# A convolution stage whose opening is reordered: reciprocals from a small column, extra TensorE work, and the first sequence run through by itself

## The chip, the cores and the metric

The kernel runs on one core of a Trainium2 chip. The metric is device time in microseconds (us); ten runs of the kernel before gave a median of 1289.62 us, the lowest 1288.46, the highest 1291.89. Five engines work side by side, each through its own list of instructions in order: TensorE (PE in the profile; its weight loads are PEld), VectorE (DVE), ScalarE (ACT), GpSimd (POOL) and SyncE (SP, which here only issues DMA transfers). An engine waits on semaphores that other engines and the DMA queues raise.

## The reference

Four stages run one after the other over an array x of 8 sequences by 512 tokens by 128 features: an attention-like dynamic convolution, an FFN with weights and inputs rounded to a 4-bit format, a test-time-training attention, and a mixture of experts. Each stage adds its result to x. The change lies in the first stage only:

```python
x = layernorm(x)                                     # per token, eps 1e-5
avg = cumsum(x, axis=1) / arange(1, l + 1)           # running mean over tokens
ci  = avg in 16 heads of 8 features                  # (b*H, l, 8)
dyn, gate = split(ci @ W_pe + b_pe)                  # 31 + 31 numbers per head and token
w = softmax(stt_energy + sigmoid(gate) * dyn)        # over 31 taps, each head and token
out[t] = sum_k w[t, k] * ci[t - 30 + k]              # causal, 31 taps
v = out @ W_fc.T + x
x_in + layernorm(v, eps 1e-6) * gamma + beta
```

## The kernel before

`sequence_conv` is the first stage. It treats the eight sequences (b = 0 to 7) one after the other, each as four tiles of 128 tokens; features or (head, tap) pairs lie on the partitions, the 512 tokens along the free axis. 31 taps are held as four groups g = 0 to 3 of eight.

The steps for one sequence, with the helper that issues them and its line in the kernel before:

- `norm0` (statistics at L255 and L257, root, offset at L270) and `scaled` (L274): the layer norm. Sequences 0 and 1 take their root with ACT's Sqrt (L268), the others with a chain of 14 small DVE operations (`rsqrt`, L85 to L93).
- `means` (L285, copy at L288): running mean. Four matmuls multiply the normed tokens by `tri`, a 512 by 512 triangle that holds 1/(t+1). Two DMA steps on SP's queue (`far` L291, `base` L294) then lay the mean out again, shifted by taps.
- `gates` (matmul eg at L300, Tanh L309, Copy L310) and `taps` (matmul ev at L300): the sigmoid of the gate and the dynamic part, two groups at a time, `half_` being 0 or 1.
- `energy` (L325 writes en, L329 and L331 keep the running maximum `top`), `turn_top`, `greatest` (L341, L343), `turn_greatest`, `less` (L351): energies, their maximum over taps, and its subtraction. `weigh` (L362, L364): exponentials.
- `part_sums`, `sums`, `invert` (L384): the softmax's denominator.
- `shared` (L402, POOL) and `product` (L411, DVE): weights times shifted means, six of eight features on DVE and two on POOL. `add_up` (cv): PE sums over taps into one PSUM bank.
- `scale_down`, `project`, `norm1`, `finish`: projection, second norm (a Newton chain on POOL for all but the last sequence), gamma, addition to x. `add_beta` (L460): x plus beta on POOL, any time after `scaled`.

A loop over b holds the steady work. Iteration b multiplies sequence b, and between its products works ahead on b+1 and b+2 and finishes b-1 and b-2. A prologue ahead of the loop fills this pipeline: it takes sequence 0 to its exponentials, sequence 1 to its first two energies and all its gates, and sequence 2 to its mean, and has all norms done.

The order on the engines is mostly written out by hand: the helpers `vec`, `ten`, `act` and `gp` each chain an instruction behind the one issued before through the same helper, so the program's text fixes the order of what passes through them. Instructions that don't pass through a helper are placed by the framework. Before, `add_beta` on POOL is of that kind.

Setting up, POOL makes `inv` (token numbers, L174), which DVE turns into reciprocals (L175, 128x512), the head mask (L180, L183), `by_k` (L230, biases in another order, from two small DMAs into `rows`), `tri` (four selects, L190), `wbig` (a memset, L210, and eight products, L214), and `half` (L236). ACT's queue issues the small input DMAs, and from `by_k` the DMA of `bias` (L232); SP's queue loads x in eight pieces.

PSUM pools: `ps_e` has two banks for eg and ev; `ps_m` one for means, turns and sums; `ps_c` one for cv; `ps_p` one for the projection; `ps_w` three for the exponentials of groups 0 to 2.

Of the kernel before, what the change touches and what calls it, by code (L numbers as in the profile page):

```python
# [7 lines left out]
F32 = mybir.dt.float32  # L8
# [132 lines left out]
def sequence_conv(cx):  # L141
# [17 lines left out]
    PITCH = PAD + L + 2  # L159
    with ExitStack() as st:  # L160
# [11 lines left out]

        inv = wp.tile([P, L], F32, tag="inv", name="inv")
        nc.gpsimd.iota(inv, [[1, L]], base=1, channel_multiplier=0, allow_small_or_imprecise_dtypes=True)  # L174
        vec(nc.vector.reciprocal(inv, inv))  # L175
# [11 lines left out]

        tri = wp.tile([P, G, L], F32, tag="tri", name="tri")
        for j in range(G):
            gp(nc.gpsimd.affine_select(  # L190
                out=tri[:, j, :], in_=inv, pattern=[[1, L]], compare_op=ALU.is_ge, fill=0.0,
                base=-P * j, channel_multiplier=-1,
            ))
# [15 lines left out]
        wbig = wp.tile([P, 2, NGR, H, KK], F32, tag="wbig", name="wbig")  # L209
        nc.gpsimd.memset(wbig, 0.0)  # L210
        for s in (1, 0):
            for g in range(NGR):
                n = min(KK, KC - KK * g)
                gp(nc.gpsimd.tensor_tensor(  # L214
                    wbig[:, s, g, :, :n],
                    wrep[:, s * KC + KK * g : s * KC + KK * g + n].unsqueeze(1).to_broadcast([P, H, n]),
                    mask_h.unsqueeze(2).to_broadcast([P, H, n]),
                    ALU.mult,
                ))
# [6 lines left out]
        with nc.allow_non_contiguous_dma(reason="small biases, once"):  # L226
# [3 lines left out]
        nc.gpsimd.tensor_copy(by_k.rearrange("h k s g -> h s g k"), rows.rearrange("h s (g k) -> h s g k", k=KK))  # L230
        bias = wp.tile([P, 3, NGR], F32, tag="bias", name="bias")
        nc.scalar.dma_start(  # L232
            out=bias.rearrange("p s g -> p (s g)"), in_=by_k.rearrange("h k s g -> h (k s g)")
        )
        half = wp.tile([P, NGR], F32, tag="half", name="half")
        gp(nc.gpsimd.tensor_scalar(half, bias[:, 1, :], 0.5, None, ALU.mult))  # L236
        wfc = wp.tile([P, D], F32, tag="wfc", name="wfc")
        nc.scalar.dma_start(out=wfc, in_=ins["L0_attn_W_fc"])
        wfc_p = wp.tile([P, NJ, ND, H], F32, tag="wfc_p", name="wfc_p")
        nc.gpsimd.tensor_copy(  # L240
            wfc_p.rearrange("p j i h -> p h i j"), wfc.rearrange("p (h i j) -> p h i j", h=H, i=ND)
        )
        wfc_t = wp.tile([P, D], F32, tag="wfc_t", name="wfc_t")
        gamma = cx.bcast(wp, "L0_attn_gamma", D)
        beta = cx.bcast(wp, "L0_attn_beta", D)

# [12 lines left out]
        def norm0(lo, hi):  # L259

            at = slice(lo * G, hi * G)
            for b in range(lo, hi):
                stats(grp(cx.x, b), mv0[:, b * G : (b + 1) * G, :])
            rs = rs0[:, at]
            if lo:
                rsqrt(nc, wp, mv0[:, at, 1], 1e-5, rs, (hi - lo) * G, vec)
            else:
                act(nc.scalar.activation(rs, mv0[:, at, 1], AF.Sqrt, bias=cx.eps[1e-5]))  # L268
                vec(nc.vector.reciprocal(rs, rs))
            vec(nc.vector.scalar_tensor_tensor(off0[:, at], mv0[:, at, 0], -1.0, rs, ALU.mult, ALU.mult))  # L270
# [7 lines left out]
        def means(b):  # L278

            avg = p2.tile([P, PITCH], F32, tag="avg", name="avg", bufs=3)  # L280
            nc.gpsimd.memset(avg[:, :PAD], 0.0)
            nc.gpsimd.memset(avg[:, PAD + L :], 0.0)
            av = ps_m.tile([P, L], F32, tag="m", name="av")
            for j in range(G):
                ten(nc.tensor.matmul(  # L285
                    av[:, j * P :], xn[:, b * G + j, :], tri[:, j, j * P :], start=(j == 0), stop=(j == G - 1)
                ))
            act(nc.scalar.copy(avg[:, PAD : PAD + L], av))  # L288
            base = p2.tile([P, DH, LB], F32, tag="base", name="base")
            far = dram.tile([P, PITCH], F32, tag="far", name="far")  # L290
            nc.sync.dma_start(out=far, in_=avg)  # L291
            for d in range(DH):
                src = bass.AP(far.tensor, far.offset + d * PITCH, [[DH * PITCH, H], [1, KK], [1, LB]])
                last = nc.sync.dma_start(out=base[:, d, :], in_=src)  # L294
            return dict(b=b, avg=avg, base=base, spread=last)

        def spread(s, i, g, name):
            e = ps_e.tile([P, L], F32, tag="e", name=name)
            now = s["avg"][:, PAD : PAD + L]
            ten(nc.tensor.matmul(e, wbig[:, i, g].rearrange("p a b -> p (a b)"), now, start=True, stop=True))  # L300
            return e

        def gates(s, half_):

            s["sg"] = {}
            for g in (2 * half_, 2 * half_ + 1):
                e = spread(s, 1, g, "eg")
                s["sg"][g] = sg = p2.tile([P, L], F32, tag="sg", name="sg", bufs=4)
                act(nc.scalar.activation(sg, e, AF.Tanh, bias=half[:, g : g + 1], scale=0.5))  # L309
                act(nc.scalar.activation(sg, sg, AF.Copy, bias=0.5, scale=0.5))  # L310

        def taps(s, half_):

            s["ev"] = {g: spread(s, 0, g, "ev") for g in (2 * half_, 2 * half_ + 1)}

        def values(s, half_):
            gates(s, half_)
            taps(s, half_)
# [139 lines left out]
        def add_beta(b):  # L458
            x = grp(cx.x, b)
            nc.gpsimd.tensor_tensor(x, x, beta.unsqueeze(1).to_broadcast([P, G, D]), ALU.add)  # L460


        norm0(0, 2)
        scaled(0)
        warm = wp.tile([P, 1], F32, tag="warm", name="warm")
        act(nc.scalar.activation(warm, cx.eps[1e-5], AF.Tanh))
        seq = {0: means(0)}
        gates(seq[0], 0)
        scaled(1)
        taps(seq[0], 0)  # L470
        norm0(2, 5)
        for g in (0, 1):
            energy(seq[0], g)
        values(seq[0], 1)
# [3 lines left out]
        seq[1] = means(1)  # L478
        for g in (2, 3):
            energy(seq[0], g)  # L480
        turn_top(seq[0])
        values(seq[1], 0)
        greatest(seq[0])
        turn_greatest(seq[0])
        scaled(2)
        norm0(5, B)
        for g in (0, 1):
            energy(seq[1], g)
        less(seq[0])
        gates(seq[1], 1)  # L490
        weigh(seq[0], 0, 1)
        seq[2] = means(2)
        taps(seq[1], 1)
        weigh(seq[0], 1, NGR)
        scaled(3)
        for b in range(B):
# [10 lines left out]
            add_up(cur, 0)  # L507
            if nxt:
                for g in (2, 3):
                    energy(nxt, g)  # L510
# [15 lines left out]
            if old:  # L526
                norm1(old, nc.gpsimd)
            if b + 4 < B:
                scaled(b + 4)
            product(cur, 2)  # L530
            add_up(cur, 2)
# [963 lines left out]
```

## Time and profile before

| what | value |
| --- | --- |
| median of ten runs | 1289.62 us |
| the profiled execution, its own time | 1292.55 us |
| its span in the profile | 1290.8 us |
| mean granted TensorE clock | 0.953 of full |
| first product on DVE (L411), sequence 0 | 45.23 us |
| first product of sequences 1, 2, 3, 4, 5 | 71.08, 97.83, 124.17, 150.51, 175.85 us |
| last product of sequence 7 begins | 239.80 us |
| busy over the whole span: PE, DVE, ACT, POOL | 85%, 59%, 38%, 57% |

A line of the timeline shows start, duration, engine, source line, operation, what it writes and reads, and how many alike were merged; a bracket at its end tells how long the engine was idle before and what ended that. A line of the windows shows, for a stretch of time, each engine's busy time with instruction counts, then the granted TensorE clock, the DMA share and GB/s. The convolution takes about the first 256 us of the span.

### The profile page before, as it was taken

The page shows a single profiled execution, that of the slowest core. Times are in us where ns is not written, and L with a number is a line of the kernel's source. Part 1 is how long each engine was busy: PE and PEld are TensorE (multiplying, and loading weights), DVE is VectorE, ACT ScalarE, POOL GpSimd, SP SyncE. Part 2 cuts the span into 40 slices and gives each one's busy share as a digit, 9 for nine tenths or more (in the row PEclk, how much of TensorE's full clock was granted, in tenths as well). Part 3 has the DMA queues.
Part 4 walks back from the last instruction along what each step waited for, and adds up shares of the span by engine and source line. Part 5 has one row for each costly group of instructions (what it writes and reads, how often), then busy time and mean ns, then how long its engine had stood idle before and what let it go on. Part 6 is the DMA issues. An engine that isn't in the chain of part 4 may idle for free.

```text
span 1290.8 us, 15323 instructions
## 1 busy us (share of the span) xinstructions
PE 1094.4 (85%) x5211; PEld 648.6 (50%) x5211; DVE 755.2 (59%) x1742; ACT 493.9 (38%) x1005; POOL 741.7 (57%) x724
## 2 busy tenths in 40 slices
PE   5899997546876699999998999999999991999990
PEld 2333442224655345555556455555576661676770
DVE  6899999687985544444445444444456873222234
ACT  4656555155556522222234223222343330333330
POOL 4347756635554688888840888888401665354542
PEclk9899999868999999999999999999999995899995
DMA  5223426660000000000000000000000112112137
GB/s 158 77 78 107 123 79 198 225 204 1 1 1 1 0 1 1 1 1 1 1 1 1 1 0 1 0 1 1 1 1 7 44 43 65 45 55 65 50 107 206
DMA packets 61615, 63.07 MB, mean 49 GB/s; under 512 B 6768, under 2 KB 44479, under 8 KB 61537
## 3 DMA queue, kind: packets, MB, share of 16 engines
q1 hardware_dynamic: 54016, 52.37, 13.8%
q0 software_dynamic: 4608, 8.43, 2.1%
q10 hardware_dynamic: 2912, 1.29, 0.5%
q8 instruction: 41, 0.67, 0.2%
q14 instruction: 38, 0.30, 0.1%
HBM read 37.90 MB, written 25.04 MB: 49 GB/s over the span
## 4 chain that ended last, share of the span: by engine, by line
PE 49%; DVE 13%; issue 5%; ACT 5%; POOL 5%; DMA 2%; SPq 0%; POOLq 0%; DVEq 0%; ACTq 0%
PE ph L1135 5%; PE sum L1110 4%; PE pp L1125 4%; PE sum L1109 4%; PE sum L1111 4%; PE pa L1087 4%; PE po L1420 4%; PE pb L1089 4%; PE ph L1411 4%; PE pt L1118 2%; PE gu L692 2%; POOL res L1435 1%; POOL v L619 1%; DVE ht L915 1%; PE a L975 1%
## 5 line engine op out<-in xcount | busy, mean ns | idle before, releaser
L1100 POOL TENSOR_TENSOR ds<-sw,s 128x512 f32<-128x512 f32 x64 | 81.5, 1274 | 87.1 <-DVE sw L1095 87.1
L1435 POOL DMA_INDIRECT res<-ye,xe x70 | 68.1, 973 | 88.6 <-DVE ye L1433 34.6
L1102 POOL TENSOR_TENSOR ds<-ds,s 128x512 f32<-128x512 f32 x64 | 111.4, 1741 | 5.0
L1327 POOL DMA_INDIRECT rows<-xr,slot x64 | 62.7, 979 | 73.8 <-DVE rs L93 45.1
L1093 ACT COPY b<-pb 128x512 f32<-128x512 f32 x64 | 37.5, 586 | 161.5 <-PE pb L1089 161.0
L1414 ACT ACTIVATE ht<-ph,b 128x512 f32<-128x512 f32 (+1 forms) x96 | 55.8, 602 | 100.6 <-PE ph L1411 99.3
L1097 DVE TENSOR_TENSOR h<-sw,b 128x512 f32<-128x512 f32 x64 | 50.4, 787 | 70.6 <-ACT b L1093 70.3
L402 POOL TENSOR_TENSOR pr<-base,en 128x512 f32<-128x512 f32 x48 | 72.5, 1540 | 32.4 <-ACT en L364 32.4
L1101 POOL TENSOR_TENSOR ds<-sw,ds 128x512 f32<-128x512 f32 x64 | 82.7, 1292 | 5.0
L1103 POOL TENSOR_TENSOR ds<-ds,b 128x512 f32<-128x512 f32 x64 | 81.4, 1271 | 5.0
L1420 PEld LDWEIGHTS po<-w,ht 128*128 128x128 f32 (+1 forms) x640 | 76.8, 187 | 12.1 <-issue 8.8
L1125 PEld LDWEIGHTS pp<-proj,ht 128*128 128x128 f32 x512 | 67.1, 191 | 30.7 <-issue 29.3
L1411 PE MATMUL ph<-xt,w 128*128 128x512 f32 (+1 forms) x192 | 74.7, 526 | 7.8 <-DVE xt L1407 7.8
L411 DVE TENSOR_TENSOR pr<-base,w 128x3072 f32<-128x3072 f32 x24 | 79.7, 3319 | 1.7 <-ACT w L362 1.7
L1420 PE MATMUL po<-w,ht 128*128 128x128 f32 (+1 forms) x640 | 79.7, 277 | 0.0
L1120 ACT COPY ht<-pt 128x512 f32<-128x512 f32 x64 | 37.5, 586 | 102.1 <-PE pt L1118 102.1
L1095 DVE TENSOR_TENSOR sw<-pa,s 128x512 f32<-128x512 f32 x64 | 44.2, 691 | 54.2 <-ACT s L1091 54.2
L1429 DVE TENSOR_TENSOR ye<-po,b 128x512 f32<-128x512 f32 (+2 forms) x32 | 14.9, 487 | 102.2 <-PE po L1420 102.2
L1137 DVE TENSOR_TENSOR db<-ph,sw 128x512 f32<-128x512 f32 x64 | 44.2, 691 | 47.1 <-PE ph L1135 47.1
L420 PE MATMUL cv<-pr,sel 128*32 128x512 f32 x512 | 63.6, 625 | 9.6 <-DVE pr L411 9.2
L1135 PE MATMUL ph<-proj_t,dpt 128*128 128x512 f32 x128 | 71.6, 641 | 0.0
L1087 PE MATMUL pa<-gate,kt 128*128 128x512 f32 x128 | 66.8, 604 | 3.3 <-ACT b L1093 3.2
(324 smaller groups left out, 2590.8 us busy)
## 6 DMA issues: line engine op xcount, KB each, us to landing
base<-far SPq DMA_DIRECT2D x64, 268.0 KB, 5.2
rows<-empty SPq DMA_DIRECT2D x1, 5005.0 KB, 17.9
xe<-rows SPq DMA_DIRECT2D x8, 585.0 KB, 4.3
res<-zero SPq DMA_DIRECT2D x1, 4096.0 KB
w<-in_L_ffn_W SPq DMA_DIRECT2D x16, 256.0 KB, 4.8
y<-res SPq DMA_DIRECT2D x16, 256.0 KB, 5.4
far<-avg SPq DMA_DIRECT2D x8, 272.0 KB, 2.1
x<-in_L_attn_x SPq DMA_DIRECT2D x8, 256.0 KB, 4.9
```

Source lines behind the costliest of these rows:

```text
L402: gp(nc.gpsimd.tensor_tensor(pr[:, d, :], s["base"][:, d, at], s["en"][:, g, :], ALU.mult))
L411: vec(nc.vector.tensor_tensor(s["pr"][g][:, :nv, :], s["base"][:, :nv, at], w.to_broadcast([P, nv, L]), ALU.mult))
L1087: nc.tensor.matmul(pa, ki, gate, start=True, stop=True)
L1100: nc.gpsimd.tensor_tensor(ds, sw, s, ALU.mult)
L1101: nc.gpsimd.tensor_tensor(ds, sw, ds, ALU.subtract)
L1102: nc.gpsimd.tensor_tensor(ds, ds, s, ALU.add)
L1103: nc.gpsimd.tensor_tensor(ds, ds, b, ALU.mult)
L1125: nc.tensor.matmul(pp, ht[:, c * P : (c + 1) * P], proj[:, c, :], start=(c == 0), stop=(c == NF - 1))
L1135: nc.tensor.matmul(ph, dpt, proj_t, start=True, stop=True)
L1411: nc.tensor.matmul(ph[:, :n], self.w1[:, e, c * P : (c + 1) * P], xt[:, :n], start=True, stop=True)
L1420: nc.tensor.matmul(po[:m, i - c0, :], ht[:, c, at : at + m], self.w2[:, e, c, :], start=(c == 0), stop=(c == NF - 1),)
L1435: sc = nc.gpsimd.indirect_dma_start(out=(self.slots.last if last else self.slots.res)[:, :], out_offset=bass.IndirectOffsetOnAxis(ap=num[: ...
```

## The change

Seven things differ, all inside `sequence_conv`:

1. The reciprocals. POOL writes token numbers by partition (`by_t`, 128x4), DVE inverts those, four matmuls against the identity spread them over all partitions, and ACT copies the result to `inv`.
2. Fourteen 128x128 matmuls of the identity with itself (`busy`) follow on PE.
3. Setting-up operations are moved: `sel` now stands ahead of the statistics on DVE, `by_k` ahead of the `wbig` memset and the second mask operation on POOL, and the issue of the `bias` DMA behind the first Sqrt on ACT. `half` stands between the two sets of `wbig` products.
4. Sequence 0's norm stands alone (`stats0`, `root`, `offset`); sequence 1's follows with a root of its own.
5. Sequence 0's four gates go to four PSUM banks of their own (`ps_w`'s three and `ps_c`'s), and its energies follow without a wait for `ps_e`.
6. What the prologue did for later sequences is moved: the roots of sequences 2 to 4 stand around `greatest` of sequence 0; the first two energies and the second half of the gates and taps of sequence 1, `scaled(2)` and `means(2)`, and the statistics and roots of sequences 5 to 7 go into iteration 0 of the loop.
7. `add_beta` is chained by `gp`: on POOL it now stands right behind the products of `shared` of its iteration.

```diff
+    BUSY = 14
-        nc.gpsimd.iota(inv, [[1, L]], base=1, channel_multiplier=0, allow_small_or_imprecise_dtypes=True)
-        vec(nc.vector.reciprocal(inv, inv))
+        by_t = wp.tile([P, G], F32, tag="by_t", name="by_t")
+        nc.gpsimd.iota(by_t, [[P, G]], base=1, channel_multiplier=1, allow_small_or_imprecise_dtypes=True)
+        vec(nc.vector.reciprocal(by_t, by_t))
+        pi = ps_c.tile([P, G, P], F32, tag="c", name="pi")
+        for j in range(G):
+            ten(nc.tensor.matmul(
+                pi[:, j, :], by_t[:, j : j + 1].to_broadcast([P, P]), cx.ident, start=True, stop=True
+            ))
+        act(nc.scalar.copy(inv, flat(pi)))
+        busy = ps_p.tile([P, P], F32, tag="p", name="busy")
+        for _ in range(BUSY):
+            ten(nc.tensor.matmul(busy, cx.ident, cx.ident, start=True, stop=True))
...
+        def root(b):
+            at = slice(b * G, (b + 1) * G)
+            act(nc.scalar.activation(rs0[:, at], mv0[:, at, 1], AF.Sqrt, bias=cx.eps[1e-5]))
+            vec(nc.vector.reciprocal(rs0[:, at], rs0[:, at]))
+        def offset(lo, hi):
+            at = slice(lo * G, hi * G)
+            return vec(nc.vector.scalar_tensor_tensor(
+                off0[:, at], mv0[:, at, 0], -1.0, rs0[:, at], ALU.mult, ALU.mult
+            ))
+        def roots(lo, hi):
+            at, n, v = slice(lo * G, hi * G), (hi - lo) * G, nc.vector
+            out, half_, sq = rs0[:, at], wp.tile([P, n], F32, tag="rh", name="half"), wp.tile([P, n], F32, tag="rq", name="sq")
+            bits = out.bitcast(I32)
+            yield vec(v.tensor_scalar(out, mv0[:, at, 1], 1e-5, None, ALU.add))
+            yield vec(v.tensor_scalar(half_, out, -0.5, None, ALU.mult))
+            yield vec(v.tensor_scalar(bits, bits, 1, None, ALU.logical_shift_right))
+            yield vec(v.tensor_scalar(bits, bits, -1.0, float(0x5F3759DF), ALU.mult, ALU.add))
+            for _ in range(3):
+                yield vec(v.tensor_tensor(sq, out, out, ALU.mult))
+                yield vec(v.tensor_tensor(sq, sq, half_, ALU.mult))
+                yield vec(v.scalar_tensor_tensor(out, sq, 1.5, out, ALU.add, ALU.mult))
+            yield offset(lo, hi)
+        stats0(0, 1)
+        root(0)
+        gp(nc.gpsimd.tensor_copy(by_k.rearrange("h k s g -> h s g k"), rows.rearrange("h s (g k) -> h s g k", k=KK)))
+        act(nc.scalar.dma_start(
+            out=bias.rearrange("p s g -> p (s g)"), in_=by_k.rearrange("h k s g -> h (k s g)")
+        ))
...
+            if s:
+                gp(nc.gpsimd.tensor_scalar(half, bias[:, 1, :], 0.5, None, ALU.mult))
...
         def add_beta(b):
-            nc.gpsimd.tensor_tensor(x, x, beta.unsqueeze(1).to_broadcast([P, G, D]), ALU.add)
+            gp(nc.gpsimd.tensor_tensor(x, x, beta.unsqueeze(1).to_broadcast([P, G, D]), ALU.add))
-        norm0(0, 2)
+        offset(0, 1)
+        stats0(1, 2)
         scaled(0)
+        root(1)
+        offset(1, 2)
...
         seq = {0: means(0)}
-        gates(seq[0], 0)
-        scaled(1)
-        taps(seq[0], 0)
-        norm0(2, 5)
+        gates(first, 0, wide)
+        gates(first, 1, wide)
+        taps(first, 0)
+        stats0(2, 5)
         for g in (0, 1):
-            energy(seq[0], g)
-        values(seq[0], 1)
+            energy(first, g)
+        taps(first, 1)
+        scaled(1)
...
-        seq[1] = means(1)
         for g in (2, 3):
-            energy(seq[0], g)
-        turn_top(seq[0])
-        values(seq[1], 0)
-        greatest(seq[0])
-        turn_greatest(seq[0])
-        scaled(2)
-        norm0(5, B)
-        for g in (0, 1):
-            energy(seq[1], g)
-        less(seq[0])
-        gates(seq[1], 1)
-        weigh(seq[0], 0, 1)
-        seq[2] = means(2)
-        taps(seq[1], 1)
-        weigh(seq[0], 1, NGR)
-        scaled(3)
+            energy(first, g)
+        turn_top(first)
+        steps = roots(2, 5)
+        for _ in range(5):
+            next(steps)
+        greatest(first)
+        seq[1] = means(1, ps_p, "p")
+        for _ in steps:
+            pass
+        turn_greatest(first)
+        gates(seq[1], 0)
+        taps(seq[1], 0)
+        less(first)
+        weigh(first, 0, 1)
+        weigh(first, 1, NGR)
         for b in range(B):
...
             add_up(cur, 0)
+            if b == 0:
+                for g in (0, 1):
+                    energy(nxt, g)
+                values(nxt, 1)
+                scaled(2)
+                then = seq[2] = means(2, ps_p, "p")
...
             add_up(cur, 1)
+            if b == 0:
+                scaled(3)
...
             product(cur, 2)
+            if b == 0:
+                stats0(5, B)
+                for _ in roots(5, B):
+                    pass
             add_up(cur, 2)
```

## The prediction

> **What bounds the kernel now.** The windows come first, over iterations 0 to 4 of the loop as their first products mark them:
>
> ```profile
> 45.20:71.10 25.90, 24.07 (x109) 9.47 (x108) 24.19 (x16) 16.05 (x29) 12.09 (x13) 0.99 0.03 12
> 71.10:97.80 26.70, 25.10 (x136) 10.82 (x134) 26.01 (x25) 13.92 (x24) 14.61 (x27) 1.00 0.32 94
> 97.80:124.20 26.40, 24.48 (x133) 10.50 (x132) 25.85 (x26) 15.20 (x28) 17.20 (x29) 1.00 0.34 94
> 150.50:175.90 25.40, 23.51 (x129) 9.93 (x129) 24.85 (x26) 13.65 (x24) 14.81 (x26) 1.00 0.36 99
> ```
>
> The third busy time is DVE's: 25.85 of 26.40 us. From 45 us on DVE sets the pace, so whatever shifts the first product of sequence 1 (71.08 us), or shortens DVE's work after it, shifts the end of the stage. Ahead of 45 us it stands still at times, as its timeline shows:
>
> ```profile
> 2.74 3.35 DVE L175 RECIPROCAL inv<-inv 128x512 f32<-128x512 f32 x1 [0.31 <-POOL inv L174]
> 9.34 3.58 DVE L270 SCALAR_TENSOR_TENSOR off<-mv,rs 128x8 f32<-128x8 f32 x1
> 22.14 0.75 DVE L325 SCALAR_TENSOR_TENSOR en<-ev,bias,sg 128x512 f32<-128x512 f32 x1 [3.22 <-ACT sg L309]
> 26.35 0.75 DVE L325 SCALAR_TENSOR_TENSOR en<-ev,bias,sg 128x512 f32<-128x512 f32 x1 [1.36 <-PE ev L300]
> 31.03 0.69 DVE L341 TENSOR_REDUCE mx<-tt 128x64 f32<-128x512 f32 x1 [1.70 <-PE tt L336]
> 36.74 1.17 DVE L93 SCALAR_TENSOR_TENSOR rs<-sq,rs 128x12 f32<-128x12 f32 x1
> 45.23 3.35 DVE L411 TENSOR_TENSOR pr<-base,w 128x3072 f32<-128x3072 f32 x1 [1.67 <-ACT w L362]
> 54.12 0.56 DVE L384 RECIPROCAL rs<-sm 128x64 f32<-128x64 f32 x1 [1.54 <-PE sm L380]
> 89.63 1.74 DVE L331 SCALAR_TENSOR_TENSOR top<-en,bias,top 128x512 f32<-128x512 f32 x1
> 168.65 0.75 DVE L331 SCALAR_TENSOR_TENSOR top<-en,bias,top 128x512 f32<-128x512 f32 x1
> ```
>
> Besides the idle time in brackets three operations are stretched: `off` at 9.34 takes 3.58 us (0.17 at 18.75), L93 at 36.74 takes 1.17 (0.17 elsewhere), L331 at 89.63 takes 1.74 where 168.65 shows 0.75. POOL's timeline tells why:
>
> ```profile
> 6.48 0.34 POOL L230 COPY by_k<-rows 16x96 f32<-16x96 f32 x1 [2.56 <-DVE s L255]
> 7.68 2.29 POOL L190 TENSOR_SCALAR_AFFINE_SELECT tri<-inv 128x512 f32<-128x512 f32 x4
> 9.96 2.94 POOL L214 TENSOR_TENSOR wbig<-wrep,mask_h 128x128 f32<-128x128 f32 x8
> 36.62 1.26 POOL L460 TENSOR_TENSOR x<-x,L_attn_beta 128x512 f32<-128x512 f32 x1 [9.00 <-ACT xn L274]
> 89.55 1.28 POOL L460 TENSOR_TENSOR x<-x,L_attn_beta 128x512 f32<-128x512 f32 x1
> ```
>
> `off` ends at 12.92, when `wbig` ends (12.90); L93 and L331 wait for `add_beta`. PE's timeline, last:
>
> ```profile
> 13.59 4.61 PE L285 MATMUL av<-tri,xn 128*128 128x512 f32 x8 [13.59 <-ACT xn L274]
> 27.34 2.32 PE L285 MATMUL av<-tri,xn 128*128 128x512 f32 x8
> 39.45 3.78 PE L300 MATMUL eg<-avg,wbig 128*128 128x512 f32 x4 [3.75 <-DVE en L325]
> ```
>
> The first mean takes 4.61 us where a later one takes 2.32; the eg at 39.45 take 3.78 against 1.96 at 18.97, behind a gap of 3.75.
>
> **The change part by part**, along the path to sequence 1's first product (before 71.08).
>
> *The reciprocal.* 3.35 us at 2.74 go; a 128x4 one costs about 0.2 (the 128x8 at 9.10). It saves the path nothing: `tri` followed POOL's `by_k`, which waits for the DMA of `rows` (landed 6.31), not for `inv` (ready at 6.09). Four matmuls, table load 1.28 and copy 0.6 on ACT follow x0's landing at 3.82 closely and are done by 6.5 to 7.6.
>
> *POOL's order.* `by_k` now stands ahead of the memset (0.94) and the second mask operation (0.19). From its start at about 6.4, 0.21 + 0.90 + 0.19 give the mask at 7.7 (before 3.92). DVE's copies into `sel` wait for it, and behind them `bn_aggr` of sequence 0: copies 0.09, aggregates 0.36, Sqrt 0.30, reciprocal 0.24 and a handover give `off` at about 8.8. `tri` begins 0.99 after `wfc_p` as before (6.69, 7.68): 8.65 (+1.0). So `off` again meets POOL, and three ends are possible: it passes at once or at the first select's end (9.0), or between `tri` and `wbig` (11.1), or only where POOL stops for `half` (8.65 + 2.29 + four `wbig` of 0.37: 12.4, ended 12.6). `bias` is issued 1.7 later and, by its 5.7 us from first issue to last landing (6.84 to 12.50), lands about 13.2 to 14.2; `half` behind it meets the first Tanh within 0.5 us in the first case, and later in none.
>
> *From `off` to the first energy*: before 12.92 to 22.14, 9.22. `busy` (14 matmuls, to about 9.7) should leave PE warm: -2.29 for av. Four eg instead of two stand before the first ev: +1.4 (1.96, less the 0.5 in which Tanh and Copy were awaited anyway). So 8.3: first energy at 17.3, 19.4 or 20.9. The second norm's pieces, `stats0(2, 5)` and the second table load (1.28) lie beside this; their cover is av and eg.
>
> *The four energies*: 22.14 to 29.33; without the 1.36 idle, 5.9.
>
> *From the last energy to product 0*: 29.33 to 45.23, 15.9. Three statistics go (31.64 to 34.88, 3.24), the roots (34.88 to 38.65, 3.77 with the stretch of 1.00), and two energies (38.65 to 41.28, 2.63). Left are 6.26, to which come roots 2 to 4: 14 steps of 0.205 = 2.9, five of them in the 1.70 of the `mx` wait, the rest while `means(1)` (2.32) runs ahead of `mb`. `less` then waits for `mb` and w for two gates on ACT (2.6): I take 8.0, between 6.3 (all covered) and 9.1 (none). Product 0 at 31.2, 33.3 or 34.8. The DMA of `base` isn't late: mean to last landing was 18.82 to 31.35, so about 25 to 29.
>
> *Iteration 0* was 25.85. Back come 2.63 + 3.24 + 2.77 = 8.64. New is a wait: energies 2 and 3 of sequence 1 need gates whose eg now stand behind `add_up(cur, 0)` on PE, itself behind POOL's products: cv 1.92 (row at 54.02), eg 1.0, Tanh 0.67, Copy 0.63 and handovers, about 4.7; it swallows the 1.54 at 54.12. Bounds: 1.5 (the old wait) and 7 (the same at half clock). Queued behind it on DVE are reciprocal and product 1. Sum 25.85 + 8.64 + 4.7 - 1.54 = 37.65. Sequence 1 begins at 68.9, 70.9 or 72.5: -2.2, -0.1 or +1.4.
>
> *`add_beta`.* Before, it met L331 at 89.55, 115.89 and 142.23 (1.74 each), and the iterations of 26.34 became 25.34 once it was gone. Now it runs right behind `shared`, beside product 1, ahead of Newton's chain, before which POOL idled 4.99 and 2.2 us: 1.28 fits. So -0.99 x 3 = -2.97. Bounds: 0 (it meets another operation) and -3.2.
>
> The Trainium skill speaks against this last term. The product's rows are 3.29 to 3.35 long whether POOL's `pr` run beside them (97.83, 3.34) or not (163.45, 3.32); only scalar_tensor_tensor was held. "GPSIMD Engine Reference" (section 1, Specifications) says that VectorE and GpSimd contend for SBUF whenever a VectorE instruction has two SBUF inputs; by that the product would be held too, up to 1.28 a time, and the term would be about +0.9 instead of -2.97. I go by the rows.
>
> **Sum**: -5.2 if `off` passes at once, -3.1 in the middle, -1.6 if it is held to 12.4. I forecast that it gets through by the end of `tri`: -4.2, the mean of the first two, against the profiled 1292.55. That execution is 2.93 over the median, the same is taken off again: 1289.62 - 4.2, about 1285.4. Its own range is 1283.4 to 1287.0. 0.2% is 2.6 us, about what a measurement here tells from no change.
>
> **Rivals.**
> - *`off` is held to 12.4.* For it: it lost some ten short operations in a row before. Against: `L331` at 49.29 (1.62) got in at POOL's next operation. -1.6: 1288.0.
> - *Slower: `off` is held through all of `wbig`* because `bias` lands early and POOL never stops. It ends at about 14.6 (+2.0 over the case before), and PE, idle from 9.7 to 15.3, is cold again (+2.29 for av): -1.6 + 4.3 = +2.7, 1292.3. It decides from an end of `off` after 14.4 with an av over 4 us. For it: the windows show clock 0.5 from 39.49 to 42.90, after 36.08 to 39.49 with 0.04 us of PE busy. Against: `bias` landed at 12.50 even when issued sooner.
> - *More gained.* The new wait in iteration 0 is 1.5 instead of 4.7 since POOL and ACT are ahead there: -7.4, 1282.2. Against: `add_up` is bound to POOL's `pr`.
> - *`add_beta` brings nothing*, the rest holds: -1.2, 1288.4.
> - *It doesn't do what it says*: PE cold at av despite `busy`. In the middle case -3.1 + 2.29 = -0.8. 1288.8.
>
> On the gap before av the trace and a page can be weighed. The gap of 3.75 us ahead of 39.45 cost the clock. "TensorE: Matmul & The Clock Gate" (Part 1) has a free-running window of about 3.4 us and full speed after one busy window. By this the gap from 9.7 to 11.6 in the middle case leaves av warm, and that from 9.7 to 13.1 only by luck of the window.
>
> **How the numbers follow.** Forecast 0.48; held to 12.4 0.18; slower 0.13; more gained 0.13; `add_beta` nothing or av cold 0.08. Faster by over 0.2% (below 1287.0): 0.9 of the forecast's, all of "more gained" and little of the others, 0.60. Within 0.2%: the rest of the forecast, the held and the last cases, 0.27. Slower 0.13. The range reaches from "more gained", 1281.5, to the ends between the held case and the slower one, 1290.5; that leaves out most of the slower rival and few of the largest gains.
>
> **What would show it.** `off` ends by 11.2 and is under 2.4 us long; av takes about 2.3 us; first energy at 17 to 19.5; product 0 at 31 to 33.5; a DVE idle of 4 to 5 us before an energy of sequence 1 in iteration 0; sequence 1's first product at 69 to 71; L331 in iterations 1 to 3 at 0.75 to 0.99; iterations near 25.4. The prediction fails if `off` is held to 14, if PE runs at 0.5 in iteration 0, or if the moved `add_beta` stretches something else.

## The result, and the profile after

The changed kernel is slower: a median of 1295.25 us over 8 runs (1294.6 to 1298.78) against 1289.65 us over 28 runs of the kernel before, a ratio of 1.0047 with a 95% interval of 1.0038 to 1.0056 (it is formed from the fast runs of both kernels and is not quite the quotient of the medians, 1.0043). The prediction was 1285.4 us with a range to 1290.5. The profiled execution took 1296.56 us (span 1294.8) where that of before took 1292.55.

Where the time went can be read off a few marks. The second profile of the kernel before belongs to the experiment e8; its own time was 1289.56 us, close to the median.

| mark (us) | before, first profile | before, second | after |
| --- | --- | --- | --- |
| first energy on DVE | 22.14 | 21.63 | 23.57 |
| first product of sequence 0 | 45.23 | 44.71 | 37.16 |
| first product of sequence 1 | 71.08 | 70.20 | 74.54 |
| first product of sequence 6 | 202.19 | 201.28 | 205.61 |
| last product of sequence 7 | 239.80 | 236.30 | 241.91 |
| end of the convolution | 256.68 | 253.47 | 260.07 |

The first product does come 8 us earlier, but iteration 0 takes 37.38 us for 25.85, and from there on nothing is gained: sequences 1 to 6 take 131.07 us after and 131.11 before. DVE's timeline after (start, duration, operation, idle time before it in brackets):

```profile
7.82 4.75 DVE L203 COPY sel<-mask_h 128x16 f32<-128x16 f32 x2 [3.21 <-POOL mask_h L196]
8.04 4.53 DVE L236 BATCH_NORM_AGGREGATE mv<-s 128x2 f32<-128x6 f32 x4
13.24 0.16 DVE L250 SCALAR_TENSOR_TENSOR off<-mv,rs 128x4 f32<-128x4 f32 x1
23.57 0.75 DVE L359 SCALAR_TENSOR_TENSOR en<-ev,bias,sg 128x512 f32<-128x512 f32 x1 [4.76 <-ACT sg L343]
37.16 3.35 DVE L445 TENSOR_TENSOR pr<-base,w 128x3072 f32<-128x3072 f32 x1 [2.28 <-ACT w L396]
48.92 0.75 DVE L359 SCALAR_TENSOR_TENSOR en<-ev,bias,sg 128x512 f32<-128x512 f32 x1 [5.25 <-ACT sg L343]
93.04 0.75 DVE L365 SCALAR_TENSOR_TENSOR top<-en,bias,top 128x512 f32<-128x512 f32 x1
104.89 1.46 DVE L365 SCALAR_TENSOR_TENSOR top<-en,bias,top 128x512 f32<-128x512 f32 x1
```

The offset that took 3.58 us now takes 0.16. What is held instead stands ahead of it: the copies into `sel`, for 4.75 us, and behind them the aggregates of sequence 0. POOL's timeline after shows the same 12.5 us as their end:

```profile
7.60 0.19 POOL L196 TENSOR_SCALAR_AFFINE_SELECT mask_h<-mask_h 128x16 f32<-128x16 f32 x1
7.74 0.40 POOL L299 COPY wfc_p<-wfc 128x128 f32<-128x128 f32 x1
8.74 2.29 POOL L278 TENSOR_SCALAR_AFFINE_SELECT tri<-inv 128x512 f32<-128x512 f32 x4
11.01 1.51 POOL L288 TENSOR_TENSOR wbig<-wrep,mask_h 128x128 f32<-128x128 f32 x4
14.66 0.24 POOL L295 TENSOR_SCALAR half<-bias 128x4 f32<-128x4 f32 x1 [2.14 <-DMA bias<-by_k]
```

The copies come free at 12.56, when POOL stops behind its fourth `wbig`. Sqrt (12.70) follows, then on ACT's queue the issue of `bias` (12.77), then the offset. PE's timeline after:

```profile
4.43 4.72 PE L188 MATMUL busy<-ident 128*128 128x128 f32 x28
14.08 4.09 PE L319 MATMUL av<-tri,xn 128*128 128x512 f32 x8 [4.92 <-ACT xn L308]
66.17 3.78 PE L334 MATMUL eg<-avg,wbig 128*128 128x512 f32 x4 [3.49 <-DVE en L359]
```

The extra matmuls end at 9.15. By 14.08 PE has stood still for 4.92 us and av is as long as in the second profile of before (4.12). (The profile lists each of these matmuls twice, so x28 stands for 14 and x8 for 4. "Cold", here and below, means at about half clock: the granted clock was 0.57 from 14.1 to 18.1 us.)

### The profile page after: what moved, and what is told of

Same layout as the page of the kernel before. It is cut to its first block, busy times and chain, and to the rows that moved or that the text cites. A ratio compares the mean times of both kernels' runs of the same rounds, so it can differ in the third digit from the quotient of the medians.

```text
span 1294.8 us, 15393 instructions
## 1 busy us (share of the span) xinstructions
PE 1104.2 (85%) x5247; PEld 656.6 (51%) x5247; DVE 750.1 (58%) x1744; ACT 495.8 (38%) x1008; POOL 738.7 (57%) x724
## 4 chain that ended last, share of the span: by engine, by line
PE 49%; DVE 12%; ACT 5%; issue 5%; POOL 5%; DMA 2%; SPq 0%; POOLq 0%; DVEq 0%; ACTq 0%
PE ph L1186 5%; PE sum L1161 4%; PE pp L1176 4%; PE sum L1160 4%; PE sum L1162 4%; PE pa L1138 4%; PE po L1471 4%; PE pb L1140 4%; PE ph L1462 4%; PE pt L1169 2%; PE gu L743 2%; POOL v L670 1%; POOL res L1486 1%; DVE ht L966 1%; PE a L1026 1%
## 6 DMA issues: line engine op xcount, KB each, us to landing
rows<-empty SPq DMA_DIRECT2D x1, 5005.0 KB, 18.1
```

## The experiments

The kernel before had medians of 1289.0 to 1324.5 us from one set of runs to another. So each ratio is to the kernel before of the same set, and only ratios and the marks of the convolution are compared between sets.

### The start: what is held, and what frees it

e2_sel_later takes the changed kernel and moves the copies:

```diff
-        for i in range(ND):
-            nc.vector.tensor_copy(sel[:, i, i, :], mask_h)
...
         offset(1, 2)
+        for i in range(ND):
+            vec(nc.vector.tensor_copy(sel[:, i, i, :], mask_h))
```

> The changed kernel, but DVE's two copies into sel stand behind the second offset instead of ahead of the first bn_aggr. Theory 1 (POOL's run of short operations from 7.7 to 12.5 holds back whichever DVE operation that needs the shared way to SBUF comes next): the aggregates run at about 4.7, Sqrt at 7.3, the bias DMA is issued at 7.4 instead of 12.77, and then the offset is held in place of the copy: it ends at 12.6, or at about 14.5 if bias lands before POOL's stop for half. Time 1294 to 1297, against 1295.25 of the changed kernel. Theory 2 (the wait for the late mask is the cause, the hold only its companion): offset ends at 8.2, first energy at about 18.5 instead of 23.57, time about 1290.

Measured: 0.9991 (0.9978 to 1.0004), first energy at 17.11, first product at 30.70, sequence 1 at 68.07 instead of 74.54. Its DVE timeline:

```profile
7.80 0.16 DVE L247 SCALAR_TENSOR_TENSOR off<-mv,rs 128x4 f32<-128x4 f32 x1
10.07 2.35 DVE L247 SCALAR_TENSOR_TENSOR off<-mv,rs 128x4 f32<-128x4 f32 x1
12.35 0.24 DVE L501 COPY sel<-mask_h 128x16 f32<-128x16 f32 x2
17.11 0.75 DVE L356 SCALAR_TENSOR_TENSOR en<-ev,bias,sg 128x512 f32<-128x512 f32 x1 [1.40 <-ACT sg L340]
```

My first theory fell by its number: the first offset was not held in the copy's place. It arrived at 7.80, 0.8 us ahead of `tri` (8.62), and passed although POOL was copying `wfc_p`. The hold itself is there all the same: the second offset, at 10.07, waits to 12.42, the end of `wbig`. So the copies' place decided, and it is worth 0.0056 of the time, about 7 us.

e3_pool_waits adds a wait of POOL's first select for the first offset:

```diff
+        off_first = offset(0, 1)
         for j in range(G):
-            gp(nc.gpsimd.affine_select(
+            one = gp(nc.gpsimd.affine_select(
...
+            if j == 0:
+                after(tc, one, off_first)
```

> The edit before, and POOL's first triangle select now waits for the first offset. Theory 1 (the hold): the offset gets through at 8.9 to 9.2, when POOL stands still; av begins at about 9.7 and, behind the extra matmuls, takes 2.3 to 2.6 us; first energy at 17.5 to 18.5, first product at 31 to 32 instead of 37.16; time 5 to 6 us under the changed kernel, 1289 to 1290.5. Rival: the early start is lost again in iteration 0, whose energies wait for PE and POOL: sequence 1's first product under 2 us earlier than 74.54, time over 1293.

Measured: 0.9996 (0.9985 to 1.0007), first energy at 17.37, first product at 32.28, sequence 1 at 69.67. The offset passed at 8.09 and `tri` began at 8.75 as it would have: the added wait never waited. The run is in effect a repeat of e2, with one difference. The copies into `sel` now met the second `wbig` set and took 1.81 us at 12.48, a second sight of a held copy. The ratio and a warm av (2.32) are those of the first theory, but not by the wait that it named. The first energy came just ahead of its 17.5 and the first product just behind its 32. That product is 1.6 us later than e2's because the mean of sequence 1 ran at half clock (granted 0.50 from 23.4 to 25.6, av 3.23 us for 2.32).

e9_mask_first undoes POOL's order alone (both mask operations through `gp`, so that they and the memset stand ahead of `by_k`):

```diff
-        nc.gpsimd.affine_select(
+        gp(nc.gpsimd.affine_select(
             out=mask_h, in_=ones, pattern=[[-DH, H]], compare_op=ALU.is_ge, fill=0.0, base=0, channel_multiplier=1
-        )
+        ))
...
```

> The changed kernel with one part undone: on POOL the wbig memset and the second mask operation stand ahead of by_k again, so that the mask is ready at about 4 us and not at 7.7; DVE's order is untouched, the copies into sel still stand ahead of the first aggregates. Theory 1 (the copies were held only because the late mask brought them to 7.8, where POOL's run begins): the copies take 0.2 us before 5, the first offset ends at about 8 instead of 13.4, bias is issued at about 7, first product at 30 to 32.5 instead of 37.16, ratio 0.998 to 1.0005 as with the copies moved. Theory 2 (the copies are held wherever they stand ahead of POOL's run, or the offset is held in their place): first product over 35, ratio over 1.0030.

Measured: 1.0016 (1.0005 to 1.0026), first product at 36.48. Its DVE timeline, then POOL's:

```profile
4.69 0.24 DVE L203 COPY sel<-mask_h 128x16 f32<-128x16 f32 x2
8.02 3.56 DVE L250 SCALAR_TENSOR_TENSOR off<-mv,rs 128x4 f32<-128x4 f32 x1
```

```profile
7.77 2.29 POOL L278 TENSOR_SCALAR_AFFINE_SELECT tri<-inv 128x512 f32<-128x512 f32 x4
```

The copies are free, and the offset is held in their place, because `tri` now begins 0.25 us ahead of it. So the late mask isn't the fault in itself: with the copies out of the way it keeps `tri` late enough (8.62) for the offset to pass. In these runs the first offset escaped only where nothing that can be held stood ahead of it and it reached DVE before `tri` began. The ratio fell between the two theories. It is 0.0031, some 4 us, under the changed kernel's, where the marks show 0.7 us at sequence 1 (73.87) and 1.9 at the end of the convolution (258.15). The profiled execution was the longest of its ten (1295.78, median 1292.05), and its mean of sequence 1 took 3.2 us at a granted clock of 0.60; where the rest lies no run shows.

e4_busy34 sets `BUSY = 34` in the changed kernel; e7_sel_no_busy sets `BUSY = 0` in e2's.

> The changed kernel with 34 extra matmuls instead of 14, which keep PE running until about 14 us. Theory 1 (PE was cold at av because it stood still from 9.15 to 14.08): av takes 2.3 us instead of 4.09, first energy and first product come 1.8 us earlier, time 1293 to 1294. Rival (av is paced by the four norm operations of ACT, 1.65 us, and by the weights, not by the clock): av stays over 3.3 us and the time within 0.7 us of 1295.25.

> The copies into sel behind the second offset, and no extra matmuls (14 to 0). Theory 1 (with the offset at 7.8 the extra matmuls do keep PE warm until av at 9.3): without them av takes 4.1 to 4.7 us instead of 2.42, first energy and first product come 2 to 3 us later (19 to 20, 32.7 to 33.7), ratio 0.9991 becomes 1.0005 to 1.0015. Rival (wbig and its bias gate the first eg at 12.5, so a cold av is hidden): first energy within 0.7 us of 17.1, the same ratio.

Measured: e4 1.0035 (1.0022 to 1.0049), with PE busy to 13.77 and av taking 2.39, first energy at 22.04 (1.5 earlier). Its first product came no earlier (37.32): the mean of sequence 1 ran at half clock instead (3.98 for 2.32, granted 0.56 from 29 to 32). Whether the added matmuls have a part in that no run shows; the same mean is slow in e3, e6, e9 and e12 too, which have 14. e7 1.0014 (1.0000 to 1.0029): av 4.60, the four eg 5.50 instead of 3.67, first energy at 21.74, first product 4.6 us later than e2's. The 4.6 are more than the 2 to 3 that were expected, since the eg were slow as well. No granted clock under 1.00 shows in e7's windows there (nor at the first mean of before, 4.61 us), so that PE was cold is read from the durations alone. The extra matmuls are worth that where the offset is early. Where it is late, more of them make av fast, and the profiled execution gained nothing by it at the first product. The ratio of 1.0035 against 1.0047 leaves a gain of some 1.5 us open. In this run iterations 1 and 2 were also shorter, 24.84 and 25.76 us (after: 25.70 and 26.35); why was not tried.

### Iteration 0: the norms and the wait

e5_norms_in_wait moves the late norms in the changed kernel; e6_sel_and_norms has this and e2's edit:

```diff
                 for g in (0, 1):
                     energy(nxt, g)
+                stats0(5, B)
+                for _ in roots(5, B):
+                    pass
                 values(nxt, 1)
...
             product(cur, 2)
-            if b == 0:
-                stats0(5, B)
-                for _ in roots(5, B):
-                    pass
```

> The changed kernel with one edit: in iteration 0 the statistics and roots of sequences 5 to 7 (59.36 to 65.37, 6.0 us of DVE) stand ahead of energies 2 and 3 of sequence 1, where DVE stood idle for 5.25 us, instead of behind product 2. Theory 1 (DVE's idle time and its added work are what make iteration 0 37.38 us long): iteration 0 falls to 31.5 to 33 us, the gap of 3.49 on PE before 66.17 goes with it and its eg take 1.98 instead of 3.78; time about 5 us under the changed kernel, ratio to before 0.9995 to 1.0015. Rival (iteration 0 is bound by POOL's products and by ACT's chain, DVE's place is immaterial): iteration 0 over 35.5, ratio over 1.0030.

> Both edits: the copies into sel stand behind the second offset (first energy at 17.1, first product at 30.7 in the run with that edit alone, ratio 0.9991), and the late norms in DVE's idle time of iteration 0. Theory 1: the two gains add, sequence 1's first product at 62.5 to 64, ratio 0.9945 to 0.9965, faster than the kernel before by about 5 us. Rival (an earlier start meets a DMA or POOL that is not earlier): sequence 1's first product later than 66, ratio over 0.9975.

Measured: e5 1.0026 (1.0014 to 1.0038), iteration 0 in 32.32 us; e6 0.9963 (0.9949 to 0.9978), iteration 0 in 32.34, sequence 1 at 64.80. DVE in e5:

```profile
42.57 0.98 DVE L365 SCALAR_TENSOR_TENSOR top<-en,bias,top 128x512 f32<-128x512 f32 x1
43.47 0.86 DVE L234 BATCH_NORM_STATS2 s<-x 128x6 f32<-128x128 f32 x4
49.76 0.75 DVE L359 SCALAR_TENSOR_TENSOR en<-ev,bias,sg 128x512 f32<-128x512 f32 x1
```

The idle 5.25 us are filled and iteration 0 is 5.06 shorter; the eg behind PE's gap of 3.49 (3.78 us) are back at 1.99. That is the first theory's length in both. Its ratio for e5 was missed by 0.001 (1.0026 is only 2.7 us under the changed kernel's, where iteration 0 gained 5), that for e6 was met. Sequence 1 came 0.8 us later in e6 than expected, since its first product (32.46) was 1.8 later than in e2, behind a wait of 1.65 for `mb`. The trace shows why: the mean of sequence 1 at 23.59 took 3.83 us, at a granted clock of 0.50 from 23.4 to 25.6. With the same opening it took 2.32 at 1.00 in e2 and e14, and was slow in e3 and e12 (3.23 and 3.58, 0.50). The gap ahead of it is only 2.48 us, and from 18.9 to 22.5 us PE was busy for 1.48 us in e6 and 1.41 in e2; which of the two happens no run here decides. So the marks of the first product vary by up to about 1.6 us from this alone, and an earlier or later one of that size is luck.

e8_before_again is the kernel before, unchanged.

> The kernel before, unchanged, for a second profile. If the half clock that the first profile shows from 39.49 to 42.90 belongs to that execution alone, sequence 1's first product comes 1 to 2.5 us before 71.08 and the convolution ends as much before 256.68; this would explain why the medians differ by 5.6 us where the two profiled executions differ by 4.0. Otherwise both repeat within 0.3 us.

Its marks are in the table above: sequence 1 only 0.9 us earlier, just under what the first case named, but the convolution ends 3.2 earlier. The half clock at the eg of 38.93 (3.78) was there again; the difference lies in the last iteration, where the first profile had a granted clock of 0.51 between 224 and 230 us and the second one 1.00. The windows of the two, first and second:

```profile
224.00:230.00 6.00, 5.35 (x24) 0.99 (x24) 4.46 (x3) 2.32 (x6) 6.00 (x5) 0.51 1.02 342
```

```profile
223.50:229.50 6.00, 5.08 (x44) 2.98 (x45) 5.14 (x5) 3.09 (x7) 6.00 (x5) 1.00 1.03 379
```

So the first profile was of a long execution, and the expected reason, the clock at 39.49, was not it.

### The steady iterations: where add_beta's gain went

e1_beta_alone makes the one edit in the kernel before:

```diff
-            nc.gpsimd.tensor_tensor(x, x, beta.unsqueeze(1).to_broadcast([P, G, D]), ALU.add)
+            gp(nc.gpsimd.tensor_tensor(x, x, beta.unsqueeze(1).to_broadcast([P, G, D]), ALU.add))
```

> The kernel before with one edit: add_beta is chained on POOL by gp, so it stands behind shared's products. Theory 1 (the prediction's step): the three stretched L331 of 1.74 us go and each of iterations 1 to 3 gets 0.99 shorter: about 1286.7 us, sequence 1's to sequence 6's first product in 128.1 us instead of 131.1. Theory 2 (formed from the profile after): the iteration is held at 26.34 us by a cycle through PE, ACT and POOL, so what DVE saves in one iteration comes back in the next as a longer L331 among the first energies (1.46 for 0.86) and as idle time before the reciprocal and the greatest; one iteration gains 1.0 earlier than it did, and the sum stays: 1289.1 to 1290.1 us, 131.1 us from sequence 1 to 6.

Measured: 1.0003 (0.9991 to 1.0014). Sequence 1 begins at 68.64, sequence 6 at 199.97: 131.33 us. The -2.97 isn't there. (Sequence 1 begins 1.6 us earlier than in the second profile of before, but the convolution ends with it, at 253.57 for 253.47.) In the changed kernel too the stretched L365 is gone (0.75 at 93.04) and comes back in the next iteration among the first energies (1.46 at 104.89), with an idle 0.16 before the reciprocal and 0.55 before the greatest. Something else holds the iteration at 26.33. Three edits on top of e6 looked for it. In e10_top_first, in iterations 1 to 7, tt stands ahead of cv on PE:

```diff
+            if nxt and b:
+                for g in (2, 3):
+                    energy(nxt, g)
+                invert(cur)
+                turn_top(nxt)
             add_up(cur, 0)
...
-            if nxt:
+            if nxt and not b:
                 for g in (2, 3):
                     energy(nxt, g)
...
```

> Both edits of the faster version (copies later, late norms in the wait), and in iterations 1 to 7 PE's turn of the maximum (tt) stands ahead of the cv matmuls of group 0 instead of behind them. Theory 1 (the iteration of 26.33 us is held by a cycle through PE and ACT: product 2, cv, eg, gates, exponentials, sums, projection, cv, tt, greatest, product 2): without cv's 1.9 us in that cycle the idle time of 0.55 before the greatest goes, DVE alone sets the pace and iterations 2 to 5 fall to 25.0 to 25.9; ratio 0.9930 to 0.9950, against 0.9963. Rival (DVE's own work is the whole of 26.33): the iterations stay at 26.2 to 26.4 and the ratio within 0.0008 of 0.9963.

Measured: 0.9965 (0.9953 to 0.9978), iterations 2 to 5 of 26.38 to 26.39. The idle 0.55 went, and L362 grew to 1.80: the rival's times, though DVE's own work isn't the whole of them. e11_top_first_beta_free undoes the chaining in it.

> The kernel of the run before with add_beta no longer chained, as in the kernel before the change. Theory 1 (the chaining was worth 1 us an iteration where DVE alone sets the pace, and its worth was hidden by the other cycle): three or four iterations show an L362 of about 1.7 us among the last energies and are 0.8 to 1.0 us longer than without; 2 to 3 us slower than the run before. Rival: the same within 0.8 us, and add_beta's place is worth nothing in any case.

Measured: 0.9973 (0.9962 to 0.9985); sequences 1 to 6 in 130.03 us, in e10 130.60. No loss in the iterations, and ratios within the noise of each other. e12_gates_first puts the eg of the second gates ahead of cv; e13_gates_first_beta_free is the same without the chaining:

```diff
             product(cur, 2)
-            add_up(cur, 2)
             if then:
                 for g in (0, 1):
                     energy(then, g)
                 gates(then, 1)
+            add_up(cur, 2)
+            if then:
                 taps(then, 1)
```

> Both edits of the faster version (copies later, late norms in the wait); in addition PE takes the eg of the second gates of sequence b+2 ahead of the cv matmuls of group 2 instead of behind them. Theory 1 (the iteration of 26.33 is held by the cycle product 2, cv, eg, gates on ACT, exponentials, sums, reciprocal, product 1, product 2): eg begins some 2 to 3 us earlier after product 2, the waits of 0.16 before the reciprocal and 0.55 before the greatest shrink, the first L362 is no longer 1.45, and iterations 2 to 5 fall to 25.0 to 25.8; ratio 0.9920 to 0.9945 against 0.9963. Rival (the loss in the first L362 comes back whatever is sped up, since POOL's products are bound to ACT's exponentials and move along): iterations 26.0 to 26.4, ratio 0.9950 to 0.9970.

> The run before without the chaining of add_beta. Theory 1: where DVE alone sets the pace, the chaining is worth the predicted 0.99 in about three iterations: one L362 of 1.7 in each of these, and 2 to 3 us more than the run before. Rival: less than 1 us between the two, so the predicted -2.97 has no place in any of these schedules.

Measured: e12 0.9951 (0.9937 to 0.9964) with iterations of 26.10, e13 0.9960 (0.9946 to 0.9973), sequences 1 to 6 in 129.89 and 129.35. (Sequence 1 begins at 67.93 in e13 for 64.80: the second offset was held for 3.55 us and the mean of sequence 1 took 4.47, at a granted clock of 0.50.) In its iterations e12 gave the rival's number. But its ACT timeline shows what waits:

```profile
112.89 0.67 ACT L393 ACTIVATE w<-en,bias 128x512 f32<-128x512 f32 x1
113.60 0.72 ACT L395 ACTIVATE en<-en,bias 128x512 f32<-128x512 f32 x1
117.18 0.59 ACT L319 COPY avg<-av 128x512 f32<-128x512 f32 x1 [2.86 <-PE av L316]
117.66 0.70 ACT L393 ACTIVATE w<-en,bias 128x512 f32<-128x512 f32 x1
```

The gates are earlier, and the first exponentials with them; then ACT stands 2.86 us for av, which is nearly the last work of PE in the iteration, and three groups of exponentials are queued behind. e14_mean_last changes that order on ACT, e15_mean_last_beta_free again without the chaining:

```diff
                 weigh(nxt, 0, 1)
-            if b + 3 < B:
-                seq[b + 3] = means(b + 3)
             if nxt:
                 weigh(nxt, 1, NGR)
+            if b + 3 < B:
+                seq[b + 3] = means(b + 3)
```

> The version with the gates first; in addition ACT takes the last three groups' exponentials of sequence b+1 ahead of the copy of the mean of sequence b+3 (avg), which there waited 2.86 us for PE's av, the last but one work of PE in an iteration. Theory 1 (the iteration hangs on PE's full list through this copy: av, avg, exponentials, partial sums, reciprocal): the wait on avg no longer stands before the exponentials, POOL's products and the sums come 2 to 3 us earlier, the reciprocal waits no more, and iterations 2 to 5 fall from 26.10 to 25.0 to 25.6; ratio 0.9910 to 0.9940 against 0.9951. Rival (PE's work alone fills the iteration, 24.5 of 26.3 us with its short gaps): 25.9 to 26.2, ratio 0.9945 to 0.9960.

> The run before without the chaining of add_beta. Theory 1 (once no cycle through PE and ACT holds the iteration, the stretched L362 lies on the path): iterations with an add_beta among the last energies are 0.8 to 1.0 longer than those without, and the sum from sequence 1 to 6 is 2 to 3 us longer than in the run before. Rival: under 1 us longer.

Measured: e14 0.9934 (0.9922 to 0.9947), iterations of 24.85 to 24.97, the lowest ratio of all. Its interval overlaps that of e12; the marks, 124.56 us from sequence 1 to 6 against 129.89, tell them apart. The waits are gone from DVE:

```profile
118.55 0.74 DVE L356 SCALAR_TENSOR_TENSOR en<-ev,bias,sg 128x512 f32<-128x512 f32 x1
119.33 0.99 DVE L362 SCALAR_TENSOR_TENSOR top<-en,bias,top 128x512 f32<-128x512 f32 x1
120.24 0.54 DVE L415 RECIPROCAL rs<-sm 128x64 f32<-128x64 f32 x1
120.70 3.29 DVE L442 TENSOR_TENSOR pr<-base,w 128x3072 f32<-128x3072 f32 x1
123.92 0.67 DVE L372 TENSOR_REDUCE mx<-tt 128x64 f32<-128x512 f32 x1
```

So the old iteration hung on PE's list through the copy of the mean on ACT: av, avg, exponentials, sums, reciprocal. In the changed kernel this copy had the same place, and waited 1.37 us at 101.28 ahead of three groups' exponentials. It took both edits together to show it; e14's without e12's was not run. e15: 0.9950 (0.9936 to 0.9964), sequences 1 to 6 in 125.21 us against 124.56. Even here the chaining is worth only 0.65 in the iterations, the rival's number. It is worth more ahead of them: in e15 an unchained `add_beta` at 12.60 holds the second offset for 3.62 us instead of 2.31, and sequence 1 begins at 65.41 instead of 63.13.

## Why the prediction was wrong, point by point

The steps of the sum against the profile (the forecast as the middle between its two cases; before in its first profile):

| step | forecast | after | error |
| --- | --- | --- | --- |
| the first offset ends | 10.05 | 13.40 | +3.35 |
| from there to the first energy | 8.3 | 10.17 | +1.87 |
| the four energies | 5.9 | 5.62 | -0.28 |
| to product 0 | 8.0 | 7.97 | -0.03 |
| iteration 0 | 37.65 | 37.38 | -0.27 |
| iterations 1 to 5 against 131.11 | -2.97 | -0.04 | +2.93 |

The sum -4.2 becomes +3.4, which is the end of the convolution (256.68 to 260.07). The rest of the program was 0.6 longer, which makes the 4.0 between the two profiled executions. The medians differ by 5.6 because the profiled execution of before was 2.9 over its median and that of after 1.3 over: the prediction had taken both to stand alike over their medians. (The four energies are 5.83 by the prediction's own rows, where it wrote 5.9.) Why the two differ was not tried; the second profile of before points to the clock in the last iteration.

*POOL's order: failed, and it is one of the two steps that decide.* "Copies 0.09" was the wrong term. I had the mask's 7.7 and the place of the copies ahead of the aggregates right, and had the hold as a rival, but looked for it only at the offset, since in the trace of before only scalar_tensor_tensor had been stretched. A copy with one input was held for 4.74 us. The slower rival had the right mechanism and the right second half (a late offset, PE cold), with the wrong operation and the wrong reason; its 1292.3 is short of 1295.25 by about the add_beta term. That it comes so near is in part luck: without that term it says +5.7, where the convolution grew by 3.4, and the rest of the 5.6 is the 0.6 behind the convolution and the 1.6 by which the two profiled executions differ in their distance from the medians. e2 shows the place of the copies to be the cause; that the late mask alone isn't, e9 shows.

The Trainium skill's "GPSIMD Engine Reference" (section 1, Specifications) names, beside two SBUF inputs, also VectorE instructions in a two-port mode. The runs here show a copy held (4.74 us after, 1.81 in e3); whether it ran in such a mode no run here shows. Its rule for two SBUF inputs does not speak against the `add_beta` term as the prediction had it: the products of groups 0 to 2 read only `base` from SBUF, their `w` lies in PSUM (`ps_w`). With `add_beta` at 82.98 beside it, product 1 at 82.32 took 3.30 us. The rows agree with the rule. `top<-en,bias,top`, both from SBUF, took 1.46 at 104.89 beside POOL's `pr`, while `en<-ev,bias,sg` just before it, with ev in PSUM, took 0.74. Product 3 does read both from SBUF, and in the kernel before it was POOL that waited: its `pr` at 96.57 took 2.50 us for 1.27 beside product 3. So what mattered beside these two-input operations was where their inputs lie, and not the operation's name, by which the prediction had sorted them.

*From the offset to the first energy: the size was off by av.* 4.09 instead of 2.32, +1.77. PE was cold because the offset was late. In e2, av began 0.1 us behind the last extra matmul and took 2.42; e4, with matmuls to 13.77, 2.39; e9, after 3.71 us of standing still, 3.91. The page that I weighed, "TensorE: Matmul & The Clock Gate" (Part 1), agrees with these: its window is 3.4 us, and gaps of 3.7 and 4.9 us cost the clock here. The half clock of e6 behind a gap of 2.48 us does not follow from an idle window of that length.

*The energies, the way to product 0, iteration 0: right*, to 0.3 us each, the new wait of 5.25 for 4.7 among them. The sum had product 0 come 12 to 14 us earlier, in its first two cases, and iteration 0 give 11.8 back. The second half held (11.53 measured), while product 0 came only 8 earlier; with the start as forecast, sequence 1 would have begun at 70. e5 shows that this wait and the norms behind product 2 make some 5 us of iteration 0's 11.5. One sign of failing that the prediction named did come, PE at 0.5 in iteration 0 (granted 0.50 from 66.1 to 70.0), but DVE had no idle time from 65.37 to 74.54, so it cost that iteration nothing.

*`add_beta`: failed, the other step that decides.* "The iterations of 26.34 became 25.34 once it was gone" was read off one iteration, and the next, without `add_beta` too, was 26.34 again. I took DVE's 25.85 busy of 26.40 us for the bound. PE's 24.48 stood in the same line, and stretches count as busy: part of DVE's busy time was waiting. e1 shows no gain; e12 and e14 show which order holds the iteration.

*The rival "it doesn't do what it says"* is what happened to the extra matmuls: they kept PE warm until 9.15, and av began at 14.08 on a cold one.

## What to carry to other kernels

Before a step is priced at its own duration, list what stands ahead of it on its engine and ask of each whether another engine can hold it: a copy of 0.2 us that comes into POOL's run costs as much as the step that was rescued. A stretched operation on a busy engine is worth its stretch only if the next iteration does not stretch something else; compare at least two iterations without it before the gain is multiplied. When an engine is 98% busy by a window, see which part of this is stretch, and look at the in-order list of the engine that feeds it: one copy that waits for another engine, ahead of work that doesn't need it, cost 1.2 us an iteration here (26.10 to 24.9).

## What the runs showed that was not expected

- A copy with one SBUF input was held by POOL's run of short operations: 4.74 us at 7.82, 1.81 at 12.48 in e3. The offset passed beside POOL's copy of `wfc_p` in e2 (0.16 us at 7.80). What exactly held the copy between 7.82 and the first select at 8.74 was not tried.
- Iterations 2 to 5 lay at 26.32 to 26.35 us in eight kernels that differ on DVE, on POOL and in PE's opening (the changed one, e1 to e3, e5 to e7 and e9), until PE's order was changed (26.10 in e12), then ACT's as well (24.85 to 24.97 in e14). The order of e10, also on PE, left 26.38, and e4 with its 34 extra matmuls had 25.76 in iteration 2.
- Two executions of the same program ended the convolution 3.2 us apart (256.68 and 253.47), with the clock at 0.51 and 1.00 in one stretch of 6 us.
